# Edge counts of a two-layer graph network: gathering edges by groups of 12 target columns

## The chip, the cores and the metric

One core of a Trainium2 chip runs the kernel. The metric is device time of one execution in microseconds (us). Before the change it is 1008.47 us, the median of 3 runs (1006.94 to 1008.85). The engines are named as the profile names them: PE is TensorE (matmuls), PEld its weight loads, DVE VectorE, ACT ScalarE, POOL GpSimd, SP the queue that issues most transfers.

## The reference: what is computed

There are 625 nodes with 1024 features, and 20,000 edges (src, dst, type), sorted by dst, with 8 types. Layer 0 is an attention over edges, layer 1 a sum over types of means of neighbours, each followed by a residual and a layer norm.

```python
# layer 0
h = x @ W                                   # 625 x 1024
al, ar = h @ a[0, :D], h @ a[0, D:]
e = exp(-leaky_relu(al[src] + ar[dst], 0.1))
rowsum = segment_sum(e, src)
h_prime = segment_sum(e[:, None] * h[dst], src) / (rowsum[:, None] + 1e-5)
x = layernorm(x + elu(h_prime))
# layer 1
u = x @ root + bias
for r in range(8):
    mask = (edge_type == r)
    sums = segment_sum(x[src] * mask[:, None], dst)
    cnt = segment_sum(mask, dst)
    u = u + (sums / maximum(cnt, 1)[:, None]) @ weight[r]
z = concat([u, x], 1) @ w_gate + b_gate
x = layernorm(x + tanh(u) * z + x * (1 - z))
```

Every edge with the same (src, dst) contributes the same numbers, so the kernel never touches edges in the sums. It makes dense matrices of counts, C_r[src, dst], how often a pair occurs with type r. Layer 0 uses their sum over types, weighting by exp of the scores; layer 1 multiplies by C_r.

## The kernel before

The work is `fast` (from line 502). A scheduler places the recorded instructions of each engine, so their order follows readiness and not only the text. Nodes are held in five tiles of 128 rows, the last with 113 (`rows_of`).

**Start (lines 552 to 745).** dst, type and src of 78 x 256 edges come in on SP (677), the last 32 edges on the ACT queue (680), tile 0 of x on the ACT queue, W in eight chunks on SP (`load_w0`). VectorE turns them to two numbers an edge: the src, and a key that is type x window + (dst - first column of the window) (697 to 701). Four transposes on PE (707) and two copies (709) put edge number c x 128 + p into partition p, column c of `src2` and `key2`, each number twice.

**Counts (lines 747 to 884).** There are 157 chunks of 128 edges. As dst is sorted, the dst of a chunk lie near 4c, within a window of 12 to 24 columns (`LEADS`, `WINS`); edges outside are counted in `astray`, and if there is any, a general kernel runs afterwards. `one_hots` (764) makes, for four chunks at a time, `s_hot` (128 edges x 626: edge has src s; column 626 on is one) and `m_hot` (edge has type r and dst d in the window) with one f16 comparison each on VectorE. Nine such pairs of buffers are there (`HOTS`). `counts_of` (782) takes 64 dst columns at a time: for each of five src tiles it fills a bank of PSUM with 8 types x 64 columns by one matmul per chunk that can meet these columns, 1,030 in all, and ACT copies each bank into `cj` (803). For every 128 columns, `all_types` sums over types on VectorE and `store_counts` writes `cd` in DRAM, eight transfers by SP. `h_of` (747) computes h of a tile by 32 matmul passes; the loop at 855 places it between groups 0, 2, 4 and 6 of ten. `row_sums` (757) forms al and ar on VectorE from h. After group 7, ar is spread over all partitions (876, `p_ar`, and ACT's copy to `ar_b`); `scores_of` (820) then needs it, al and the counts.

**Attention (lines 887 to 1031).** `turn_scores` transposes scores on PE (843, `patt`) and ACT copies them to `attT`; `gather_h` (653, `phh`) multiplies with h for all 25 pairs of tiles. `attend` adds, normalizes and stores the new x, `turned_pieces` transposes and splits it in three pieces (h, l, d).

**Dense passes (from line 946).** `dense_tile` does x1 @ matrix in split precision, three matmuls per chunk (952, 953, 956), weights of 128 columns from the pieces, 512 columns of fp32r streamed. They run for root, the eight `weight[r]`, and the gate's two halves. For each r and half, 50 matmuls (1114, `pu`) multiply with the counts, fetched again from `cd`. The counts of edges per (dst, type) are the row of ones of `cd` (1059), cast by ACT (1060) and transposed (1065).

The few lines that a sentence can't say are those of the count matmul:

```python
nc.tensor.matmul(
    p3[:, :, lo - d0:hi - d0], s_hot[:k, c % BC, t * 128:(t + 1) * 128],
    m_hot[:k, c % BC, :R * win].rearrange("p (r w) -> p r w", r=R)[:, :, lo - base:hi - base],
    start=(i == 0), stop=(i == len(parts) - 1), skip_group_check=True)
```

Of the kernel before, what the change touches and what calls it, by code (L numbers as in the profile page):

```python
# [437 lines left out]

F32R = mybir.dt.float32r
SLOPES = 4  # L440
NC = -(-E // 128)
NROW = 78
LAST = E - NROW * 256
BC = 4
HOTS = 9
SONE = 626
G = 64
NG = -(-N // G)
H_AFTER = (0, 2, 4, 6)
AHEAD = 3  # L450
EARLY = 3
ST = 5
SP = ST * 128
# [6 lines left out]
def lead_of(b):  # L460

    first, last = b * BC / NC, min(1, (b + 1) * BC / NC)
    q = min(max(first, 0.5), last)
    return max(4, math.ceil(4.5 * N * math.sqrt(q * (1 - q) / E)))


LEADS = [lead_of(b) for b in range(-(-NC // BC))]
WINS = [SLOPES + 2 * lead for lead in LEADS]


def rows_of(t):
    return min(128, N - t * 128)
# [30 lines left out]
def fast(  # L503
# [26 lines left out]
    ps = ctx.enter_context(tc.tile_pool(name="f_ps", bufs=8, space=bass.MemoryType.PSUM))  # L530

    def bank(name):
        return ps.tile([128, 512], F32, tag="bank", name=name)
# [14 lines left out]
    def load_row(rows, ap, name):  # L548
# [15 lines left out]
                   allow_small_or_imprecise_dtypes=True)  # L564

    wins = const.tile([1, 2, NROW], F32, name="wins")
    lead_row, win_row = wins[:, 0, :], wins[:, 1, :]
    rows0 = 0
    while rows0 < NROW:
        lead = LEADS[2 * rows0 // BC]  # L570
        rows1 = rows0
        while rows1 < NROW and LEADS[2 * rows1 // BC] == lead:
            rows1 += 1
        nc.gpsimd.memset(lead_row[:, rows0:rows1], float(lead))
        rows0 = rows1
    nc.gpsimd.tensor_scalar(win_row, lead_row, 2.0, float(SLOPES), op0=OP.mult, op1=OP.add)
    first_row = const.tile([1, NROW], F32, name="first_row")
    nc.gpsimd.iota(first_row, pattern=[[2 * SLOPES, NROW]], base=0, channel_multiplier=0,
                   allow_small_or_imprecise_dtypes=True)
    nc.gpsimd.tensor_tensor(lead_row, first_row, lead_row, op=OP.subtract)  # L580
    p_win = bank("p_win")
    for i in range(2):
        nc.tensor.matmul(p_win[:NROW, i:i + 1], wins[:, i, :], ones[:1, :1], start=True, stop=True)
    row_wins = const.tile([128, 2], F32, name="row_wins")
    nc.vector.tensor_copy(row_wins[:NROW], p_win[:NROW, :2])
    row0, row_win = row_wins[:, 0:1], row_wins[:, 1:2]
# [9 lines left out]
    src2 = const.tile([128, NC, 2], F16, name="src2")  # L596
    key2 = const.tile([128, NC, 2], F16, name="key2")
# [23 lines left out]

    def tile_cols(t):
        return slice(t * 128, t * 128 + rows_of(t))

    def move_rows(n, dma):

        r0 = 0
        for m in (128, 112, 1):
            if m <= n - r0:
                dma(slice(r0, r0 + m))  # L630
                r0 += m
        assert r0 == n

    def load_x(pool, t, name, bufs=None, eng=nc.sync, clear=False):
        xt = pool.tile([128, D], F32, tag="x", name=f"{name}_{t}", bufs=bufs)
        if clear and rows_of(t) < 128:
            nc.gpsimd.memset(xt[96:], 0.0)
        xr = x[t * 128:t * 128 + rows_of(t), :]
        move_rows(rows_of(t), lambda rows: eng.dma_start(xt[rows], xr[rows]))
        return xt  # L640
# [12 lines left out]
    def gather_h(t, j):  # L653

        n, nj = rows_of(t), rows_of(j)
        for half in range(2):
            if j == 0:
                banks_h[t, half] = bank(f"phh_{t}_{half}")
            nc.tensor.matmul(banks_h[t, half][:n, :], attT[:nj, j, t * 128:t * 128 + n],  # L659
                             h_sb[:nj, j, half * HALF:(half + 1) * HALF],  # L660
                             start=(j == 0), stop=(j == ST - 1), skip_group_check=True)

    with tc.tile_pool(name="f_w", bufs=4, side="right") as wpool, \
# [7 lines left out]
        edge_rows = free[:NROW, D:D + 768].bitcast(I32).rearrange("p (i c) -> p i c", i=3)  # L671
        pair = free[:NROW, D + 768:D + 1280].rearrange("p (i c) -> p i c", i=2)
        rel, scratch = free[:NROW, D + 1280:D + 1536], free[:NROW, D + 1536:D + 1792]
        edge_last = scores.tile([1, 3, LAST], I32, name="edge_last")
        ends = ((1, dst), (2, etype), (0, src))
        for i, ap in ends:
            nc.sync.dma_start(edge_rows[:, i, :], ap[0:NROW * 256].rearrange("(p c) -> p c", c=256))
        x_next = load_x(xin, 0, "x", eng=nc.scalar)
        for i, ap in ends:
            nc.scalar.dma_start(edge_last[:, i, :], ap[NROW * 256:E].rearrange("(p c) -> p c", p=1))  # L680
# [15 lines left out]
        for h in range(2):  # L696
            nc.vector.tensor_scalar(rel[:, h * 128:(h + 1) * 128], edge_rows[:, 1, h * 128:(h + 1) * 128],
                                    row0[:NROW], float(-SLOPES * h), op0=OP.subtract, op1=OP.add)
        nc.vector.scalar_tensor_tensor(pair[:, 1, :], edge_rows[:, 2, :], row_win[:NROW], rel,
                                       op0=OP.mult, op1=OP.add)  # L700
        nc.vector.tensor_copy(pair[:, 0, :], edge_rows[:, 0, :])
        xT_next = x_turned(0)
        pe = bank("p_edges")
        pe4 = pe[:, :4 * NROW].rearrange("p (i h q) -> p i h q", i=2, h=2)
        for i in range(2):
            for h in range(2):
                nc.tensor.transpose(pe4[:, i, h, :], pair[:, i, h * 128:(h + 1) * 128], ident[:NROW, :NROW])
        for i, dst2 in enumerate((src2, key2)):
            nc.vector.tensor_copy(
                dst2[:, :2 * NROW, :].rearrange("p (q h) w -> p h q w", h=2),  # L710
                pe4[:, i, :, :].unsqueeze(3).to_broadcast([128, 2, NROW, 2]),
            )

        def last_edges():

            bad = scores.tile([NROW, 4], F32, name="bad")
            nc.vector.memset(bad, 0.0)
            pair_l = scores.tile([1, 2, LAST], F32, name="pair_l")
            rel_l = scores.tile([1, LAST], F32, name="rel_l")
            nc.vector.tensor_copy(pair_l[:, 0, :], edge_last[:, 0, :])  # L720
            nc.vector.tensor_scalar(rel_l, edge_last[:, 1, :], float(LEADS[-1] - SLOPES * (NC - 1)), None, op0=OP.add)
            nc.vector.scalar_tensor_tensor(pair_l[:, 1, :], edge_last[:, 2, :], float(WINS[-1]), rel_l,
                                           op0=OP.mult, op1=OP.add)
            pl = bank("p_last")
            for i in range(2):
                nc.tensor.matmul(pl[:LAST, i:i + 1], pair_l[:, i, :], ones[:1, :1], start=True, stop=True)
            for i, dst2 in enumerate((src2, key2)):
                nc.vector.tensor_copy(dst2[:LAST, NC - 1, :], pl[:LAST, i:i + 1].to_broadcast([LAST, 2]))
            for i, (bound, bound_l, op) in enumerate(((0.0, 0.0, OP.is_lt), (row_win[:NROW], float(WINS[-1]), OP.is_ge))):
                nc.vector.tensor_scalar(scratch, rel, bound, 0.0, op0=op, op1=OP.add, accum_out=bad[:, i:i + 1])  # L730
                nc.vector.tensor_scalar(scratch[:1, :LAST], rel_l, bound_l, 0.0, op0=op, op1=OP.add,
                                        accum_out=bad[:1, 2 + i:3 + i])
            pb = bank("p_bad")
            nc.tensor.matmul(pb[:1, :4], ones[:NROW, 0:1], bad, start=True, stop=True)
            total = scores.tile([1, 1], F32, name="total")
            nc.vector.tensor_reduce(total, pb[:1, :4], axis=AX.X, op=OP.add)
            nc.vector.tensor_copy(astray, total)

        built = {}
# [3 lines left out]
        s_hots = [hot.tile([128, BC, SP], F16, name=f"s_hot_{i}", bufs=1) for i in range(HOTS)]  # L743
        for m in s_hots:
            nc.gpsimd.memset(m[:, :, SONE:], 1.0)

        def h_of(t, xT):
            n = rows_of(t)
            halves_h = [bank(f"ph_{t}_{half}") for half in range(2)]
# [4 lines left out]
            for half, p in enumerate(halves_h):  # L754
                nc.scalar.copy(h_sb[:n, t, half * HALF:(half + 1) * HALF], p[:n, :])
# [8 lines left out]
        def one_hots(b):  # L764

            if b in built:
                return built[b]
            c0, n = b * BC, min(BC, NC - b * BC)
            k = 128 if c0 + n < NC else LAST
            if k == LAST:  # L770
                assert n == 1
            made = s_hots[b % HOTS], hot.tile([128, BC, R * max(WINS)], F16, tag="m_hot", name=f"m_hot_{b}")
# [82 lines left out]
        for g in range(NG):  # L855
# [5 lines left out]
            if g == 0:  # L861
                last_edges()
# [360 lines left out]
```

## Time and profile before

| what | us |
|---|---|
| median of 3 runs | 1008.47 |
| the profiled execution | 1009.31 |
| its span on the core | 1007.5 |
| from the start to the first count matmul | 0 to 24.8 |
| counts, and h of tiles 1 to 4 | 24.8 to 152.3 |
| attention, up to the first dense matmul | 152.3 to 196.8 |
| root passes | 196.8 to 256.1 |
| eight types | 256.1 to 878.4 |
| gate passes and end | 878.4 to 1007.5 |
| count matmuls (pc), busy | 62.4 |
| one-hots on VectorE, s_hot and m_hot, busy | 57.1 and 19.6 |

Times in views are us from the start of the span, unless marked ns. A group's line gives engine, operation, what is written and read, its shape and the number of instructions; then the busy time, the mean of one in ns, and the idle time of the engine just before them with what ended it. Instructions of one engine overlap in its pipeline, so the step from one start to the next can be shorter than the duration. The chain of waits is followed back from the last instruction to whatever released each; a piece counts both weight loads and matmuls. The TensorE clock was granted in full in each of these stages; the first matmuls ran at half pace (h passes of 854 ns until 13.3 us, 429 ns afterwards).

### The profile page before, as it was taken

Reading aid. Unit: us, or ns where it says so; the run is one execution under the profiler, and the core shown is the slowest. Engines: PE = TensorE matmul, PEld = TensorE weight load, DVE = VectorE, ACT = ScalarE, POOL = GpSimd, SP = SyncE. Lnnn points to the kernel's source line nnn. Section 1 sums busy time; section 2 is a strip of 40 time slices with the busy share of each in tenths; the row PEclk is TensorE's granted clock in tenths of the full one; section 3 lists DMA queues with packets and bytes.
Section 4 is the critical chain, followed back from the end, with each engine's and each line's share of the span. In section 5 each row is a group of like instructions: output and inputs, shape, how many; then the busy total and the mean of one; then the engine's idle time right before and its main releaser. Section 6 shows DMA issues by size and latency. Waiting matters only on the chain.

```text
span 1007.5 us, 12429 instructions
## 1 busy us (share of the span) xinstructions
PE 986.5 (98%) x4899; PEld 773.9 (77%) x4899; DVE 610.2 (61%) x948; ACT 393.4 (39%) x710; POOL 33.8 (3%) x72
## 2 busy tenths in 40 slices
PE   8999999999999999999999999999999999999994
PEld 4667774587888888888888888888888888888874
DVE  7477769876564563562653653644645635639995
ACT  1322337633445244343343442551551541423422
POOL 1000000100000000000000000000000000002123
PEclk9999999999999999999999999999999999999997
DMA  7022336453220220310310310311301202342212
GB/s 280 22 72 53 81 110 199 146 155 117 84 84 21 96 83 2 116 63 22 116 63 21 117 62 23 116 41 43 107 31 63 84 1 83 101 130 84 83 41 105
DMA packets 60951, 83.65 MB, mean 83 GB/s; under 512 B 28877, under 2 KB 29119, under 8 KB 60886
## 3 DMA queue, kind: packets, MB, share of 16 engines
q1 hardware_dynamic: 60735, 82.27, 25.5%
q8 instruction: 40, 0.66, 0.3%
q10 hardware_dynamic: 150, 0.52, 0.1%
q14 instruction: 26, 0.20, 0.1%
HBM read 71.11 MB, written 11.67 MB: 82 GB/s over the span
## 4 chain that ended last, share of the span: by engine, by line
PE 94%; DVE 3%; ACT 1%; issue 0%; DMA 0%; POOL 0%; SPq 0%; POOLq 0%; DVEq 0%; ACTq 0%
PE pu L1114 19%; PE p_w L956 14%; PE p_w L953 14%; PE p_w L952 14%; PE ph L752 7%; PE pc L799 5%; PE phh L659 4%; PE p_root L952 2%; PE p_root L956 2%; PE p_root L953 2%; PE p_wgx L956 2%; PE p_wgx L953 2%; PE p_wgx L952 2%; PE p_wgu L956 1%; PE p_wgu L953 1%; PE p_wgu L952 1%
## 5 line engine op out<-in xcount | busy, mean ns | idle before, releaser
L953 PE MATMUL p_w<-m_w,x_l 128*128 128x512 f32 x640 | 249.2, 390 | 0.0
L952 PE MATMUL p_w<-g_w,x_h 128*128 128x512 f32 x640 | 248.9, 389 | 0.0
L1114 PE MATMUL pu<-y,cf 128*128 128x512 f32 (+1 forms) x800 | 189.1, 395 | 0.0
L1114 PEld LDWEIGHTS pu<-y,cf 128*128 128x128 f32 (+1 forms) x800 | 150.6, 188 | 35.6
L1096 DVE SCALAR_TENSOR_TENSOR v<-p_w,v 128x512 f32<-128x512 f32 (+1 forms) x80 | 55.2, 689 | 202.1 <-PE p_w L956 153.0
L956 PE MATMUL p_w<-e_w,x_d 128*128 128x512 f32 x640 | 176.7, 390 | 0.0
L953 PEld LDWEIGHTS p_w<-m_w,x_l 128*128 128x128 f32 x640 | 120.1, 188 | 25.5 <-DVE m_w L926 0.2
L956 PEld LDWEIGHTS p_w<-e_w,x_d 128*128 128x128 f32 x640 | 120.1, 188 | 25.4 <-DVE e_w L927 0.3
L952 PEld LDWEIGHTS p_w<-g_w,x_h 128*128 128x128 f32 x640 | 120.1, 188 | 25.3
L1095 ACT ACTIVATE v<-p_w 128x512 f32<-128x512 f32 (+1 forms) x80 | 47.5, 593 | 217.2 <-PE p_w L953 217.2
L926 DVE SCALAR_TENSOR_TENSOR m_w<-raw_w,e_w 128x512 fp32r<-128x512 f32 x128 | 84.8, 683 | 36.2 <-ACT e_w L925 36.2
L1099 DVE TENSOR_TENSOR y<-v,y 128x512 fp32r<-128x512 f32 (+1 forms) x80 | 55.2, 690 | 50.8 <-ACT y L1098 50.8
L927 DVE TENSOR_TENSOR e_w<-g_w,m_w 128x512 fp32r<-128x512 f32 x128 | 84.7, 683 | 0.5
L924 ACT ACTIVATE g_w<-raw_w 128x512 fp32r<-128x512 f32 x128 | 73.1, 620 | 29.6 <-PE p_w L952 20.2
L1098 ACT CAST y<-v 128x512 fp32r<-128x512 f32 (+1 forms) x80 | 49.2, 615 | 75.2 <-DVE v L1096 75.2
L752 PE MATMUL ph<-w,xT 128*128 128x512 f32 (+1 forms) x160 | 72.8, 614 | 1.1 <-ACT xT L690 1.1
L925 ACT ACTIVATE e_w<-raw_w 128x512 fp32r<-128x512 f32 x128 | 73.0, 620 | 0.0
L799 PEld LDWEIGHTS <-s_hot 128*128 128x128 f16 x1030 | 62.0, 98 | 3.9 <-issue 3.7
L799 PE MATMUL pc<-m_hot,s_hot 128*128 128x192 f16 (+19 forms) x1030 | 62.4, 222 | 0.7 <-DVE m_hot L774 0.7
L774 DVE TENSOR_TENSOR s_hot<-iota,src 128x2504 f16<-128x2504 f16 (+1 forms) x40 | 57.1, 1429 | 9.4 <-PE pc L799 9.4
L752 PEld LDWEIGHTS ph<-w,xT 128*128 128x128 f32 (+1 forms) x160 | 30.7, 195 | 40.0 <-issue 38.0
L1118 DVE SCALAR_TENSOR_TENSOR L_gnn_bias_dram_u<-pu,inv,L_gnn_bias_dram_u 128x512 f32<-128x512 f32 (+1 forms) x80 | 55.5, 743 | 5.3 <-PE pu L1114 5.3
(155 smaller groups left out, 962.8 us busy)
## 6 DMA issues: line engine op xcount, KB each, us to landing
raw_w<-in_L_gnn_weight_dram SPq DMA_DIRECT2D x64, 512.0 KB, 3.3
cd<-cj SPq DMA_DIRECT2D x40, 160.0 KB, 3.6
cs<-cd SPq DMA_DIRECT2D x8, 800.0 KB, 5.6
w<-in_L_gnn_W_dram SPq DMA_DIRECT2D x8, 512.0 KB, 5.5
raw_root<-in_L_gnn_root_dram SPq DMA_DIRECT2D x8, 512.0 KB, 3.3
raw_wgx<-in_L_gnn_w_gate_dram SPq DMA_DIRECT2D x8, 512.0 KB, 3.4
raw_wgu<-in_L_gnn_w_gate_dram SPq DMA_DIRECT2D x8, 512.0 KB, 3.2
x<-in_x_dram SPq DMA_DIRECT2D x7, 512.0 KB
```

The lines of the kernel that those rows point to most:

```text
L752: nc.tensor.matmul(p[:n, :], xT[:, k, :n], w0_sb[k][:, half * HALF:(half + 1) * HALF], start=k == 0, stop=k == KC - 1)
L774: nc.vector.tensor_tensor(m[:k, :n, :width].rearrange("p c (j w) -> p c j w", w=2), iota16[:k, :width].rearrange("p (j w) -> p j w", w=2). ...
L799: nc.tensor.matmul(p3[:, :, lo - d0:hi - d0], s_hot[:k, c % BC, t * 128:(t + 1) * 128], m_hot[:k, c % BC, :R * win].rearrange("p (r w) -> ...
L924: nc.scalar.activation(g, w, AF.Copy, scale=DOWN)
L925: nc.scalar.activation(e, w, AF.Copy, scale=UP12 * DOWN)
L926: nc.vector.scalar_tensor_tensor(m, w, UP12, e.bitcast(F32), op0=OP.mult, op1=OP.subtract)
L927: nc.vector.tensor_tensor(e, g.bitcast(F32), m.bitcast(F32), op=OP.subtract)
L952: nc.tensor.matmul(p1[:n, :], h[:, k, :], g, start=k == 0, stop=False, skip_group_check=True)
L953: nc.tensor.matmul(p1[:n, :], l[:, k, :], m, start=False, stop=k == KC - 1, skip_group_check=True)
L956: nc.tensor.matmul(p2[:n, :], d[:, k, :], e, start=k == 0, stop=k == KC - 1, skip_group_check=True)
L1114: nc.tensor.matmul(p, c[:m, t, j * 128:(j + 1) * 128], piece[:m], start=(t == 0 and i == 0), stop=(t == ST - 1 and i == 1), skip_group_che ...
L1118: nc.vector.scalar_tensor_tensor(at, p[:n], inv[:n, j, r:r + 1], at, op0=OP.mult, op1=OP.add)
```

## The change

**Tiles.** All five tiles have 125 rows. Count matrices keep columns of 128 per tile, the last three clear. Matmuls and transposes use 125 rows and columns. Each transfer of a tile's rows is two now: 112 rows and 13.

**Start.** All edges come as 125 x 160, dst, src, type, two transfers each. VectorE packs each edge into one number, (dst x 40 + src tile x 8 + type) x 128 + src within its tile, in five operations; ACT's queue writes them to DRAM (`packed`, 627 rows of 32 with padding at both ends). For each of 55 groups of dst columns (eleven per tile, of 12 columns, the last of 5) a comparison of every 32nd dst and six small matmuls (`p_count`) tell at which block of 32 it begins. Eight indirect transfers on the POOL queue fetch for each group 16 blocks, as four chunks of 128 edges. `place_edges`, after seven of the eight steps of h of tile 0, transposes them, and four VectorE operations make `src2` and `key2`.

**Counts.** `s_hot` is 126 wide (src within its tile, whichever the tile; the last column is one), and `m_hot` has (dst column, src tile, type), 40 per dst column. One bank holds 12 dst columns x 40. A group takes four matmuls (two for the short one), 210 in all; chunks have fixed windows of columns 0 to 6, 1 to 11, 5 to 12 and 8 to 12. There are 15 builds of up to four groups, six comparisons each, five pairs of buffers. h of tiles 1 to 4 is cut in 32 steps, spread over the first 38 groups; x of a tile is transposed in the middle of h of the tile before. row sums, sums over types, the spread of ar and the first scores are put on a list with a due group each. PSUM has six banks for all else and two for h until the counts are done, then eight.

**Later.** The counts of edges per (dst, type) are the sum of five rows of `cd`, added on VectorE. Their total against 20,000 gives `astray` (a matmul `p_all`), in place of the four checks at the start.

The diff, cut to its core:

```diff
-SLOPES = 4
-NC = -(-E // 128)
...
-BC = 4
-HOTS = 9
-SONE = 626
-G = 64
-H_AFTER = (0, 2, 4, 6)
+TN = N // ST
+BLOCK = 32
+NBLOCK = E // BLOCK
+GCOLS = 12
+NG = -(-TN // GCOLS)
+NGS = ST * NG
+TR = ST * R
+LO = 128
+ONE = TN + 1
+BG = 4
+HOTS = 5
+H_GROUPS = 38
+LAG = 4
...
 def rows_of(t):
-    return min(128, N - t * 128)
+    return TN
...
-    ps = ctx.enter_context(tc.tile_pool(name="f_ps", bufs=8, space=bass.MemoryType.PSUM))
+    begin = ExitStack()
+    ps = [begin.enter_context(tc.tile_pool(name="f_ps0", bufs=6, space=bass.MemoryType.PSUM))]
+    ps_h = begin.enter_context(tc.tile_pool(name="f_ps_h", bufs=2, space=bass.MemoryType.PSUM))
...
     def move_rows(n, dma):
         r0 = 0
-        for m in (128, 112, 1):
-            if m <= n - r0:
-                dma(slice(r0, r0 + m))
-                r0 += m
+        for m in (n // 16 * 16, n % 16):
+            dma(slice(r0, r0 + m))
+            r0 += m
...
+        less = scores.tile([TN, per // BLOCK, 2 * NGS], F16, name="less")
+        nc.vector.tensor_tensor(
+            less, samples.unsqueeze(2).to_broadcast([TN, per // BLOCK, 2 * NGS]),
+            thr[:TN].rearrange("p g h -> p (g h)").unsqueeze(1).to_broadcast([TN, per // BLOCK, 2 * NGS]), op=OP.is_lt)
...
+        nc.vector.tensor_scalar(rest, edge_rows[:, 0, :], 1.0 / TN, 0.5 / TN - 0.5, op0=OP.mult, op1=OP.add)
+        nc.vector.tensor_scalar(rest, rest, MAGIC, MAGIC, op0=OP.add, op1=OP.subtract)
+        nc.vector.scalar_tensor_tensor(pack, rest, float(LO * R - TN), edge_rows[:, 0, :], op0=OP.mult, op1=OP.add)
+        nc.vector.scalar_tensor_tensor(pack, edge_rows[:, 1, :], float(LO * TR), pack, op0=OP.mult, op1=OP.add)
+        nc.vector.scalar_tensor_tensor(pack, edge_rows[:, 2, :], float(LO), pack, op0=OP.mult, op1=OP.add)
...
+        move_rows(TN, lambda rows: nc.scalar.dma_start(packed_rows[rows], pack[rows]))
+        p = bank("p_count")
+        for m in range(per // BLOCK):
+            nc.tensor.matmul(p[:2 * NGS, :1], less[:, m, :], ones16[:TN], start=m == 0, stop=False)
...
+        for b in range(2):
+            for i in range(4):
+                nc.gpsimd.indirect_dma_start(edges[:, b, i, :], None, packed[:, :],
+                                             bass.IndirectOffsetOnAxis(ap=at_block[:, b, i:i + 1], axis=0))
...
+        def place_edges():
+            pe = bank("p_edges")[:, :4 * NGS]
+            for b in range(2):
+                nc.tensor.transpose(pe[:, b * 2 * NGS:(b + 1) * 2 * NGS], edges[:, b].rearrange("p i c -> p (i c)"),
+                                    ident[:2 * NGS, :2 * NGS])
...
+            for b in range(-(-len(wins) // 2)):
+                equal(s_hot[:, b, :i1 - i0, :, :ONE].rearrange("p g h c -> p (g h) c"),
+                      src2[:, b, i0:i1].rearrange("p g h w -> p (g h) w"), ONE)
+            at = 0
+            for j, (first, end) in enumerate(wins):
+                width = TR * (end - first)
+                equal(m_hot[:, :i1 - i0, at:at + width], key2[:, j // 2, i0:i1, j % 2, :], width)
+                at += width
...
+        def counts_of(i, cj):
+            g = i % NG
+            s_hot, m_hot, _ = built[i]
+            p = bank(f"pc_{i}")
+            at = 0
+            for j, (first, end) in enumerate(WINS[g]):
+                nc.tensor.matmul(p[:, TR * first:TR * end], s_hot[:, j // 2, j % 2, :],
+                                 m_hot[:, at:at + TR * (end - first)],
+                                 start=j == 0, stop=j == len(WINS[g]) - 1, skip_group_check=True)
+                at += TR * (WINS[0][j][1] - first)
+            nd = cols_of(g)
+            nc.scalar.copy(cj.rearrange("s t r d -> s (t r) d")[:, :, g * GCOLS:g * GCOLS + nd],
+                           p[:, :TR * nd].rearrange("s (d q) -> s q d", q=TR))
...
+        for i in range(NGS):
+            while steps < min(n_steps, (i + 1) * n_steps // H_GROUPS):
+                next(h_steps, None)
+                steps += 1
+                if steps % KC == 0:
+                    due.append((i + (LAG if steps < n_steps else 0), row_sums, steps // KC))
+                    if steps == n_steps:
+                        due.append((i + 6, lambda _: spread_ar(), None))
...
+            counts_of(i, cjs[-1])
+            if i % NG == NG - 1:
+                due.append((i + LAG, counted, i // NG))
...
     def dense_tile(t, chunks, name):
-        n = 128
+        n = rows_of(t)
...
-    nc.sync.dma_start(ins16[:, :N], cd[:, SONE - 4 * 128, 4, :N])
-    nc.scalar.copy(ins[:, :N], ins16[:, :N])
+    nc.sync.dma_start(ins16, cd[:, ONE, :, :])
+    nc.vector.tensor_tensor(ins, ins16[:, 0, :], ins16[:, 1, :], op=OP.add)
+    for t in range(2, ST):
+        nc.vector.tensor_tensor(ins, ins16[:, t, :], ins, op=OP.add)
...
+    nc.vector.tensor_reduce(in_r, ins, axis=AX.X, op=OP.add)
+    p = bank("p_all")
+    nc.tensor.matmul(p[:1, :1], in_r, ones[:R, :1], start=True, stop=True)
+    nc.vector.tensor_scalar(astray, p[:1, :1], -1.0, float(E), op0=OP.mult, op1=OP.add)
```

## The prediction

> **What bounds the kernel now.** I read the page's busy line first, then the chain of work that ended last, then busy time by stage, then groups of instructions, then single stretches of the timeline.
>
> ```profile
> PE 986.5 (98%) x4899; PEld 773.9 (77%) x4899; DVE 610.2 (61%) x948; ACT 393.4 (39%) x710; POOL 33.8 (3%) x72
> ```
>
> TensorE (PE) is busy nearly all the time, but 98% is a mean; the chain says whether it is also what ends last where the change works (columns: start, length, what).
>
> ```profile
> 1.60 4.28 DMA attT<-in_src_dram
> 8.25 16.58 PE ph L752 x32
> 24.83 4.48 PE pc L799 x90
> 30.91 14.00 PE ph L752 x32
> ...
> 130.89 5.49 PE pc L799 x87
> 152.28 7.92 PE phh L659 x18
> ...
> 265.50 1.81 PE p_w L956 x8
> ```
>
> From 8 us on the chain is TensorE alone: products h (ph) and counts (pc) in turn, then the attention sum (phh), then the dense passes. So in this stretch a microsecond of TensorE is worth a microsecond, until another engine takes over. By stage (columns: window, length, busy PE, PEld, DVE, ACT, POOL, clock, DMA):
>
> ```profile
> 24.80:152.30 127.50, 125.12 (x1217) 90.85 (x1213) 86.17 (x111) 38.97 (x70) 0.60 (x1) 1.00 0.25 67
> 152.30:196.80 44.50, 44.50 (x126) 21.08 (x127) 42.17 (x73) 32.46 (x62) 4.24 (x7) 1.00 0.51 170
> ```
>
> In the count stage VectorE (DVE) has 41 us to spare, in the attention stage 2. The first dense product starts at 196.84; all sums below run up to that start, because what follows keeps its instructions.
>
> **The change part by part.** Rows that price it:
>
> ```profile
> L799 PE MATMUL pc<-m_hot,s_hot 128*128 128x192 f16 (+19 forms) x1030 | 62.4, 222 | 0.7 <-DVE m_hot L774 0.7
> L774 DVE TENSOR_TENSOR s_hot<-iota,src 128x2504 f16<-128x2504 f16 x39 | 56.7, 1453 | 9.4 <-PE pc L799 9.4
> L803 ACT CAST cj<-pc 128x512 f16<-128x512 f32 x45 | 26.4, 586 | 30.5 <-PE pc L799 30.5
> L659 PEld LDWEIGHTS phh<-h_sb,attT 128*128 128x128 f32 x64 | 11.8, 190 | 13.6 <-issue 11.7 <-ACT attT L845 1.3 <-ACT cj L803 0.2
> L659 PEld LDWEIGHTS phh<-h_sb,attT 128*113 128x113 f32 x16 | 2.8, 178 | 3.5 <-issue 3.5
> ```
>
> ```profile
> 9.68 1.44 DVE L774 TENSOR_TENSOR s_hot<-iota,src 128x2504 f16<-128x2504 f16 x1
> 11.05 0.34 DVE L774 TENSOR_TENSOR m_hot<-iota,key 128x384 f16<-128x384 f16 x1
> 11.31 1.45 DVE L774 TENSOR_TENSOR s_hot<-iota,src 128x2504 f16<-128x2504 f16 x1
> ```
>
> *Counts on TensorE, -37.7 us.* Away go 1,030 matmuls over 131,120 columns, 62.4 us. In come 50 groups of four (240, 400, 280, 160 columns) and 5 short ones (200, 160): 210 matmuls, 55,800 columns. Price between 0.442 ns a column (1.81 us for eight of 512, the chain's p_w piece) and 0.476 (62.4 / 131,120, which holds many narrow ones). The new ones are wide, so 0.442: 24.7 us (at most 26.6).
>
> *Interleaving, +2.8.* The changed program's order has 31 switches from counts to an h matmul before the last h; before there were none without transposes between. Where five 40-column counts (151.98) precede a phh (152.21) about 0.09 us goes beyond their streaming. 31 x 0.09 = 2.8. Bounds: 0, and 0.24 each (7.4), the gap before an h that waits for ACT's copy.
>
> *Turning x earlier, -1.5.* The four gaps before h (0.24 us, ACT's xT copy) fall away, with the six p_last and p_bad matmuls (0.44).
>
> *Start, +3.0.* Edges now come as six transfers, spaced about 0.4 us, then wait for a VectorE chain: the last is issued at 2.4, and lands 4.28 later (the chain's first line), 6.7. The order on VectorE puts the compare for the block counts behind the packing: five ops of 160 elements after the source ids, the last after the types (0.25 to 0.35 each, by the rows of 128 and 256 elements), compare of 550 elements 0.64, done 8.2. TensorE has the count of blocks (0.85, as p_win's four took 0.69) ahead of the x transposes, and ACT the write of the packed copy ahead of the xT copies. So transposes start at 9.1 instead of 4.29, h at 11.0 instead of 8.05. Below 2 or above 4.5 I don't expect it.
>
> *Gather, 0.* The packed write leaves at 7.6 and lands by 11.9 (4.28 again). Eight gathers on GpSimd follow; no row shows one. Bounds: 0.31 us each, SP's shortest issue of an edge load, and 4.28 each, one wholly after another. A gather of 110 rows is issued like a transfer, but by GpSimd, whose longest one-off op before this stage's end took 0.95; I take 0.95: 11.9 + 7.6 + 3.9 = 23.4. TensorE needs the edges after seven eighths of h of tile 0, at 11.0 + 14.8 = 25.8 (16.58 less an eighth of a warm h, 1.75); that h is the cover. From 1.25 us each the wait shows: at 4.28 the edges come at 46.1, +20.3. Behind the waiting transposes stand the rest of h and all counts.
>
> [...]
>
> *VectorE, 0 until the last h.* From the timeline an element of a one-hot costs (1.37 - 0.26) / (2504 - 384) = 0.523 ns, an instruction 0.06 us. Before: 124,618 elements, 80 instructions, 70 us. After: 27,720 + 59,400 = 87,120 elements, 90 instructions, 51 us. It starts later: at 27.9 instead of 9.7 (25.8, transposes 0.4, four key ops on 220 and 440 elements 1.6). Up to the last one-hot it also has four row sums (2.5 us each) and three sums over types (2.5): 51 + 10 + 7.5 ends at 96.4 if never waiting. TensorE's last h ends at 27.6 + 0.4 + 3.5 (turns) + 56.0 (four h) + 37 groups x 0.45 + 2.8 = 107. So it hides, with 10 us of cover.
>
> *A new stall, +5.3.* Before, three of ten groups' counts (17 us) stood between the last h and the first attention transposes and covered row sums, ar's spread and the first scores. Now 18 short groups, 8.1 us, stand there. The road from the last h: two copies 1.4, row sums 2.5, p_ar 0.6, ACT behind seven evictions and two copies to 5.8; then VectorE's 1.40 (types of tile 3) and six score ops of 0.735, one of 0.74, one more 0.8: first turned scores at 12.2; with ACT's copies behind a pair of weight casts phh begins at 14.0. Idle: 14.0 - 8.1 - 0.6 of transposes = 5.3. Next late would be the pieces of x1 for the first dense tile. TensorE has 46.9 us from phh's begin (100 passes at 0.429, 36 transposes at 0.109). VectorE has, from there, 14.9 us of scores and types, 18 weight pieces and small ops 12.3, three tiles of x1 13.1, the pieces 2.4: 42.7. They stay hidden by 4 us, as before by 3 (ready at 193.0, used from 196.0). ACT's evictions now write runs of 12 in another order; no row shows that form: 0.586 by the old one; twice that would add 11 here.
>
> *Tiles of 125, 0.* Instructions keep their count and width in the free dimension. 3,440 dense and aggregation matmuls lose 3 of 128 weight columns. The load shrinks with columns (190 to 178 ns for 113), 2.4 ns for 3, and lies beneath a 227 ns matmul. Bounds: -8.3 us if the load sets the pace, and +24 if an uneven layout costs the 6.9 ns by which pu (11.66 us for 50) exceeds p_w.
>
> [...]
>
> *Edges' sums later, +0.3.* Four VectorE adds and a reduction (3.7 us) stand in place of one ACT cast; the load came 7.8 us before its use, and that slack covers them; the p_all matmul remains. The 28 extra transfers (112 + 13 rows) go to SP, which waits hundreds of us for free buffers; without that cover some 0.4 us each.
>
> Sum: 3.0 - 37.7 + 2.8 - 1.5 + 5.3 + 0.3 = -27.8. The profiled execution took 1009.31 (span 1007.5), 0.84 above the median of 1008.47: 981.5 for it, 980.7 for the median.
>
> **Rivals.** [...] (2) *ACT takes over after the last h* with slow evictions: for: runs of 12; against: ACT is 30% busy. 992. (3) *125 columns cost*: for: pu's 6.9 ns; against: equal ph pace at 113 and 128 columns (429 ns). 1004. (4) *Slower*: the one-hots lose VectorE's f16 pace, as smaller blocks with another layout. f32 rows cost 0.735 us for 640 elements, 1.15 ns, over twice 0.523. At twice, +45.6; 10 hidden, 35.6 - 27.8 = +7.8: 1016. It decides from 38 us more, 0.96 ns an element. Against: every operand stays f16 in pairs. (5) *Better*: the load sets the pace: 972.
>
> **How the numbers follow.** Forecast 0.60, gather 0.16, ACT 0.07, columns 0.05, one-hots 0.05, better 0.07. The likeliest gives 981, its own range 974 to 988. To leave out no more than 2 in 10: 971 to 996. What a measurement here can tell from no change is about 0.2%, 2 us. Slower takes the one-hot case and two of the columns', 0.07; within 0.2%, 0.02; faster the rest, 0.91.
>
> **What would show it.** pc near 25 us in 210 matmuls; h at about 11; p_edges transposes without a wait; the last h near 107; a gap of some 5 us before phh; the first dense matmul near 169; p_w still at 227 ns. Wrong if TensorE waits at p_edges, if VectorE is full before the last h, or if p_w's pace moved.

## The result and the profile after

The changed kernel took 994.81 us (median of 4 runs, 993.65 to 995.49), the kernel before beside it 1007.81 (1006.94 to 1008.85): 0.9869 of it, 95% interval 0.9852 to 0.9886. It is 13.0 us faster. The forecast was 981, a gain of 27.8; the time lies inside the stated 971 to 996, close to the upper end, and 13.0 of the 27.8 us came. The profiled execution took 993.65, its span is 991.8.

The first view is the chain of work that ended last (start, length, what).

```profile
2.03 4.02 DMA attT<-in_src_dram
8.09 6.26 DMA packed<-attT
24.81 3.20 DMA edges<-packed,at_block
28.39 2.76 PE ph L773 x4
...
120.01 1.98 PE phh L678 x4
...
253.83 1.87 PE p_w L1016 x8
255.70 11.67 PE pu L1182 x50
...
293.50 1.87 PE p_w L1016 x8
295.36 11.67 PE pu L1182 x50
```

Two things are to be seen. At the start the chain runs through the packed copy and the gather (it did not before), and the edges land at 28.0. In the dense part eight products in a row take 1.87 us; they took 1.81 before. The aggregation (pu) takes 11.67, as before. From one pu to the next there are 39.67 us in place of 38.90. The chain of the kernel before:

```profile
283.64 11.66 PE pu L1114 x50
322.54 11.66 PE pu L1114 x50
```

The groups of instructions say the same (out<-in, weights rows*columns, count, then busy time and mean ns of one). The first line is of the kernel before, the others are of after, the counts (pc) among them:

```profile
L956 PE MATMUL p_w<-e_w,x_d 128*128 128x512 f32 x640 | 176.7, 390 | 0.0
...
L1182 PE MATMUL pu<-y,cf 125*125 125x512 f32 x800 | 189.2, 394 | 0.0
...
L823 PE MATMUL pc<-m_hot,s_hot 128*128 128x240 f16 (+2 forms) x210 | 29.5, 277 | 0.0
...
L1016 PE MATMUL p_w<-e_w,x_d 128*125 128x512 f32 x640 | 180.3, 394 | 0.0
```

The mean of a p_w record is 394 ns (390 before); the records are pipelined, so the pace is read from the starts: 233.3 ns from one p_w matmul to the next, 226.7 before (most frequent steps 233 and 234 against 227 and 226). In the same way the 210 count matmuls, busy for 29.5 us by their records, take 24.1 us from each start to the next start on TensorE; the 1,030 before took 62.0.

Stages by the same borders as in the forecast, in us:

| | before | after | difference |
|---|---|---|---|
| start to the first dense product | 196.84 | 166.84 | -30.0 |
| first dense product to the end | 810.7 | 825.0 | +14.3 |
| of this, 16 half passes over a type | 16 x 38.90 | 16 x 39.67 | +12.3 |
| span | 1007.5 | 991.8 | -15.7 |

(The medians differ by 13.0 and not by 15.7, because the profiled execution of before was 1.5 above the median of its runs now and that of after 1.2 below its own.) So the stage that the change rewrites gained 2.2 us more than forecast, and the stage of which the forecast said that nothing changes gave 14.3 back. The 2.2 is no more than scatter: of six profiled kernels with this same front (after and five of the kernels below) the first dense product starts between 166.75 and 169.21, and the forecast was 169.04.

What TensorE waited for in the whole of the execution after (engine, line, releaser: us in total, times, longest):

```profile
PE p_count L730 <- DVE less L717: 8.8, 1, 8.8
PE patt L869 <- DVE e L859: 2.8, 1, 2.8
PE p_edges L747 <- DMA edges<-packed,at_block: 2.3, 2, 1.6
PE p_wgu L1016 <- DVE e_wgu L985: 1.4, 2, 0.9
PE phh L678 <- ACT attT L871: 0.4, 1, 0.4
```

No count waits for a one-hot, the gather is late by 2.3 us, and the stall behind the last h is 2.8 + 0.4.

### The profile page after: what moved, and what is told of

Read it like the earlier page. It is cut to its first block, busy times and chain, and to the rows that moved or that the text cites. A ratio compares the mean times of both kernels' runs of the same rounds, so it can differ in the third digit from the quotient of the medians.

```text
span 991.8 us, 10873 instructions
## 1 busy us (share of the span) xinstructions
PE 964.9 (97%) x4075; PEld 721.4 (73%) x4075; DVE 596.0 (60%) x955; ACT 391.5 (39%) x714; POOL 43.5 (4%) x73
## 4 chain that ended last, share of the span: by engine, by line
PE 93%; DVE 3%; DMA 1%; POOL 1%; ACT 1%; issue 1%; SPq 0%; POOLq 0%; ACTq 0%; DVEq 0%
PE pu L1182 19%; PE p_w L1016 15%; PE p_w L1012 15%; PE p_w L1013 15%; PE ph L773 6%; PE phh L678 4%; PE p_root L1016 2%; PE p_root L1012 2%; PE p_wgx L1013 2%; PE p_root L1013 2%; PE p_wgx L1016 2%; PE p_wgx L1012 2%; PE pc L823 2%; PE p_wgu L1016 1%; PE p_wgu L1013 1%; PE p_wgu L1012 1%
## 5 line engine op out<-in xcount | busy, mean ns | idle before, releaser
L1012 PE MATMUL p_w<-g_w,x_h 128*125 128x512 f32 x640 | 252.0, 394 | 0.0
L1013 PE MATMUL p_w<-m_w,x_l 128*125 128x512 f32 x640 | 252.0, 394 | 0.0
L1182 PE MATMUL pu<-y,cf 125*125 125x512 f32 x800 | 189.2, 394 | 0.0
L1016 PE MATMUL p_w<-e_w,x_d 128*125 128x512 f32 x640 | 180.3, 394 | 0.0
L1182 PEld LDWEIGHTS pu<-y,cf 125*125 125x125 f32 x800 | 148.1, 185 | 38.5
L1013 PEld LDWEIGHTS p_w<-m_w,x_l 128*125 128x125 f32 x640 | 118.5, 185 | 31.1 <-DVE m_w L984 0.2
L1016 PEld LDWEIGHTS p_w<-e_w,x_d 128*125 128x125 f32 x640 | 118.4, 185 | 31.2 <-DVE e_w L985 0.2
L1012 PEld LDWEIGHTS p_w<-g_w,x_h 128*125 128x125 f32 x640 | 118.4, 185 | 30.7
L773 PE MATMUL ph<-w,xT 128*125 128x512 f32 x160 | 78.9, 622 | 0.0
L1186 DVE SCALAR_TENSOR_TENSOR L_gnn_bias_dram_u<-pu,inv,L_gnn_bias_dram_u 125x512 f32<-125x512 f32 x80 | 55.5, 742 | 7.9 <-PE pu L1182 7.9
```

What stands on the lines that cost most here:

```text
L773: nc.tensor.matmul(p[:n, :], xT[:, k, :n], w0_sb[k][:, half * HALF:(half + 1) * HALF], start=k == 0, stop=k == KC - 1)
L1012: nc.tensor.matmul(p1[:n, :], h[:, k, :n], g, start=k == 0, stop=False, skip_group_check=True)
L1013: nc.tensor.matmul(p1[:n, :], l[:, k, :n], m, start=False, stop=k == KC - 1, skip_group_check=True)
L1016: nc.tensor.matmul(p2[:n, :], d[:, k, :n], e, start=k == 0, stop=k == KC - 1, skip_group_check=True)
L1182: nc.tensor.matmul(p, c[:m, t, j * 128:j * 128 + n], piece[:m], start=(t == 0 and i == 0), stop=(t == ST - 1 and i == 1), skip_group_check ...
L1186: nc.vector.scalar_tensor_tensor(at, p, inv[:n, j, r:r + 1], at, op0=OP.mult, op1=OP.add)
```

## The experiments

### Is it the 125 weight columns?

*wide* clears (on GpSimd) the three spare columns of every piece and uses all 128 as weights in the dense matmuls.

```diff
+        for i in (h, l, d):
+            nc.gpsimd.memset(i[:, :, n:].bitcast(F32), 0.0)
-            nc.tensor.matmul(p1[:n, :], h[:, k, :n], g, ...)
+            nc.tensor.matmul(p1, h[:, k, :], g, ...)
```

> The changed kernel with the three spare columns of each piece of x1 and u cleared by GpSimd, and all 128 used as weights in the 2,640 dense matmuls; the aggregation (pu) stays at 125. Columns theory (125 weight columns cost each dense matmul 233.3 - 226.9 = 6.4 ns): eight second products in a row take 1.81 us again instead of 1.87, 16.9 us go, some 978 us. Rival (the dense passes are slower for another reason: more transfers, the earlier start, the clock): the pace stays at 1.87 and the time at 995.

979.98 us (5 runs), 0.9726 of before [0.9712, 0.9741]: 14.8 less than the changed kernel. *widepu* does the same for the aggregation, where the spare columns of the counts are zero already.

```diff
-                p = banks_u[j][:n]
+                p = banks_u[j]
-    nc.tensor.matmul(p, c[:m, t, j * 128:j * 128 + n], piece[:m], ...)
+    nc.tensor.matmul(p, c[:m, t, j * 128:(j + 1) * 128], piece[:m], ...)
```

> The kernel of the run above, with 128 weight columns in the 800 aggregation matmuls (pu) too; the last three columns of the counts are zeros. If their 233.3 ns after the change is the price of 125 columns, as the dense ones', up to 800 x 6.4 = 5.1 us more go, some 973 us, and 50 take about 11.35 us. If they are slow for their own reason, as before the change with 128 columns (11.66 for 50), nothing more goes: 978 us.

976.25 us, 0.9686 [0.9666, 0.9705]: 3.7 more (in the traces half a pass falls from 38.88 to 38.59 us, 16 of them 4.6). The chains of both, *wide* first:

```profile
254.12 1.81 PE p_w L1018 x8
255.93 11.66 PE pu L1184 x50
```

```profile
251.96 1.81 PE p_w L1018 x8
253.77 11.36 PE pu L1184 x50
```

The pace follows the edit, line by line: 1.87 to 1.81 for the dense products with the first, 11.66 to 11.36 for the aggregation with the second. Neither more transfers nor the earlier start nor the clock is needed, and three more columns, all zeros, are worth 18.6 us together. In this code the weight columns of a product are also the rows that it writes in PSUM (`p1[:n, :]`), so the edit widens both; no run separates the two. The theory stands so far; that each matmul of 125 columns has its price does not follow yet.

### Is it a price of each matmul?

*before125* takes the kernel before and leaves the last three columns out of seven dense matmuls in eight.

```diff
+            w = 125 if k else 128
-            nc.tensor.matmul(p1[:n, :], h[:, k, :], g, ...)
+            nc.tensor.matmul(p1[:w, :], h[:, k, :w], g, ...)
```

> The kernel before, whose dense matmuls use the first 125 columns from k = 1 on (the products of the last three rows of each tile are left out there): this part of the change alone. Columns theory: 2,640 x 7/8 = 2,310 matmuls at 6.4 ns are 14.8 us more, 1022 us. Rival (it only costs together with the rest of the change): 1008.

1010.01 us, 1.0026 [1.0017, 1.0036]. Only 2.4 of 14.8 us came, so the price for each matmul falls. *k0wide* is the other side of it: the changed kernel with 128 columns for k = 0 alone.

> The changed kernel, of whose dense matmuls only those with k = 0, one in eight, use 128 weight columns; the others stay at 125. If each matmul with 125 columns costs 6.4 ns: 330 x 6.4 = 2.1 us less than the changed kernel, 993 us. If the slow pace is a lock that one wider matmul breaks (before, with 125 columns from k = 1 on, gained only 2.4 us in place of 14.8): most steps at 227 ns, some 981 us.

985.03 us, 0.978 [0.9765, 0.9795]: one matmul in eight, made wider, takes away 9.8 of the 14.8 us. In the profiled executions, from the first dense product to the end, it is 12.2 of 15.6 (824.9 us after, 812.7 here, 809.4 in *wide*). The chain of *k0wide* inside one pass (the first three lines are the first tile of a pass, where three kinds of product alternate, the others two later tiles):

```profile
620.19 0.23 PE p_w L1020
620.43 0.23 PE p_w L1015
620.66 0.23 PE p_w L1016
...
627.56 1.81 PE p_w L1020 x8
633.00 1.81 PE p_w L1020 x8
```

By the records, a pass there has some twenty steps of 233 ns in the first tile and then steps of 227 to its end, for the same 125 columns. In *before125* four steps in five are 226 or 227 as well. So the same 125-column product goes at either pace. Not every wider matmul ends the slow one: the three at the head of the first tile have 128 columns too, and the pace changes only where the second tile begins.

*widths* changes the columns of the second product alone (k from 1 on), beside neighbours of 128; in *purewidths* all dense matmuls of one type have one width.

```diff
+    WID = [128, 127, 126, 125, 124, 120, 112, 96]
+        w = wid_of(name)
+        h, l, d = (i[:, :, :w] for i in x1[t])
```

> The kernel with 128 dense columns, but the second product of type r uses, from k = 1 on, only the first 128, 127, 126, 124, 120, 112, 96 and 64 columns of its weights for r = 0 to 7 (the rest of those products is left out). If 128 alone is fast, the eight second products in a row take 1.81 us for type 0 and some 1.87 for all others. If odd numbers, or numbers that 4 or 16 do not divide, are slow: 1.87 for 127 (and 126, 124, 120 as far as it goes) and 1.81 for the rest. If the load's length counted, they would grow shorter with the columns.

> The kernel with 128 dense columns; in the dense matmuls of type r all weights have 128, 127, 126, 125, 124, 120, 112 and 96 columns for r = 0 to 7 (the products of the other rows are left out, and so are those rows in the aggregation of that type). Theory A (only 128 columns are fast): 227 ns for type 0, 233 or more for all others. Theory B (the pace is a lock between load and matmul, which some widths fall into): as in the mixed run, 227 for 128, 127 and 124, and some 233 for 126, 125 and 120.

980.96 and 987.99 us, one execution each, so only the steps inside them are read. The mean step from start to start, in ns, from the records of p_w (128 of *purewidths* is its second half pass, as the first holds single steps of up to 338):

| columns | 128 | 127 | 126 | 125 | 124 | 120 | 112 | 96 | 64 |
|---|---|---|---|---|---|---|---|---|---|
| all matmuls of the pass (*purewidths*) | 226.8 | 233.3 | 233.3 | 233.3 | 226.8 | 233.3 | 229.0 | 230.1 | - |
| seven in a row (k from 1) among 128 (*widths*) | 226.7 | 226.7 | 233.6 | - | 226.7 | 233.3 | 228.9 | 230.0 | 230.0 |

The chain of *purewidths*, one line each from the types with 128, 127 and 125 columns:

```profile
277.07 1.81 PE p_w L1023 x8
...
316.20 1.87 PE p_w L1023 x8
...
474.84 1.87 PE p_w L1023 x8
```

127 columns are slow by themselves and fast beside 128; 124 are as fast as 128 in both; 120 are slower than 112; and 64 columns are no faster than 128. So neither "only 128 is fast" nor "fewer columns, shorter load" holds, and theory B fails on 127. What the runs show for 120 to 128 columns is a pace of a whole run of matmuls, near 226.7 or near 233.3, that goes on until something breaks it, and into which some widths fall; 112 to 64 columns lie between, at 229 to 230. Why these widths, and what in TensorE holds the pace, no run here tells; that stays open.

### What was the late gather worth?

*afterlate* is the changed kernel with the edges placed later: their transposes stand behind the whole h of tile 0 and the turning of tile 1, and six steps of h come before the first counts (the other 26 are spread over the same 38 groups).

```diff
-            if k == KC - 2:
-                place_edges()
+        place_edges()
+        for _ in range(H_FIRST):
+            next(h_steps)
```

> The changed kernel, 125 columns as it is, with nothing but the edges' transposes placed later: behind all of h of tile 0 and the turning of tile 1, six h steps ahead of the first counts. The late gather's price by itself: 2.3 us of wait, less 1.3 that the run with 128 columns still showed, and the half clock that followed it, some 1.7 us. Theory: 2.7 to 4 us less, 991 to 992 us. Rival (VectorE's one-hots begin no earlier and pace the stage): 995.

990.3 us, 0.9820 [0.9807, 0.9834]: 4.5 less, a little over the upper end of what was expected. Timelines of TensorE, after and then *afterlate* (start, length, instruction, and the wait ahead of it in brackets):

```profile
26.17 0.29 PE L747 MATMUL p_edges<-ident,edges 110*128 110x110 f32 x1 [0.64 <-DMA edges<-packed,at_block]
28.11 0.28 PE L747 MATMUL p_edges<-ident,edges 110*128 110x110 f32 x1 [1.65 <-DMA edges<-packed,at_block]
28.23 2.92 PE L773 MATMUL ph<-w,xT 128*125 128x512 f32 x4
```

```profile
24.46 3.17 PE L774 MATMUL ph<-w,xT 128*125 128x512 f32 x7
27.47 1.02 PE L668 MATMUL px<-ident,x 125*128 125x125 f32 x8
28.32 0.35 PE L748 MATMUL p_edges<-ident,edges 110*128 110x110 f32 x2
```

In the second the wait is gone. In the first, four h take 2.92 us right behind it, where four in the steady stretch start within 1.75. The windows from 28 to 33 us show why (busy PE, PEld, DVE, ACT, POOL, then the granted clock, the DMA share and GB/s), after and then *afterlate*:

```profile
28.00:33.00 5.00, 4.89 (x14) 2.87 (x15) 4.43 (x9) 2.06 (x4) 0.00 (x0) 0.66 0.00 0
```

```profile
28.00:33.00 5.00, 5.00 (x18) 2.57 (x17) 4.61 (x10) 1.22 (x3) 0.00 (x0) 1.00 0.31 102
```

The clock was at half from 28.96 to 32.37 us, 3.41 us, which costs 1.7 by estimate, half of it. Wait and clock together make 4.0, and in the traces the last h starts 4.2 earlier (103.00 against 107.18). The first dense product starts only 2.9 earlier (163.96 against 166.84), since in *afterlate* the clock was at half from 114.71 to 118.13 us, around the begin of the attention; what is left of the 4.5 lies behind that start. VectorE, whose one-hots begin no earlier, was not in the way.

*late* is the same on top of *widepu*:

> The kernel with 128 columns in dense and aggregation (976 us), with the transposes of the edges placed behind all of h of tile 0 and the turning of tile 1, and six h steps behind them ahead of the first counts. If the late gather cost the path its 2.3 us of wait and the half clock after it (4 h in 2.92 us in place of 1.75, some 1.4 us with the transposes): 3.7 us go, 972.5. Rival (VectorE's one-hots, which begin no earlier, set the pace up to the last h): 976.

971.21 us, 0.9647 [0.9634, 0.9661], 5.0 below *widepu*; 3.7 were expected.

### What stands behind the last h?

*late30* spreads h over 30 groups of counts (`H_GROUPS = 30`), *late36* over 36.

> The same, with the h steps spread over 30 groups of counts instead of 38, so that some 25 groups lie behind the last h instead of 17. If the 3.2 us that TensorE waits between the last h and the attention sum are the road from the last h (row sums, ar, scores), they are covered by 3.5 us more of counts: 970. Rival (VectorE, 11.1 of 12 us busy there, is what ends it, and only gets its one-hots later): no gain over the run above, 972.5 to 975.

978.64 us, 0.9727 [0.9714, 0.9741]: 7.4 more. The cover was there, but TensorE now waited for what makes the counts:

```profile
PE pc L824 <- DVE m_hot L800: 4.0, 3, 2.7
PE pc L824 <- ACT cj L829: 2.2, 1, 2.2
```

The clock fell behind these waits: it was at half from 113.95 to 127.60 us, 13.65 us, against 3.41 (116.61 to 120.03) in *late*. The attention sum begins 6.7 us later (122.89 against 116.20); how much of that is waits and how much clock, no run separates.

> 128 columns everywhere, edges late (971 us), with h over 36 groups in place of 38: two groups of counts more (0.9 us) behind the last h, whose road to the attention sum left TensorE idle for 2.8 us. Theory (a little of that idle time can be covered before VectorE runs out of one-hots): 970 to 971. Rival (VectorE is at its limit at 38 already, as with 30): over 972.

970.6 us, 0.9636 [0.9623, 0.9649], the best of all kernels here, but not distinguishable from *late*; the wait for the scores is still 2.8. What makes the counts becomes the limit somewhere between 36 and 30 groups. So two runs took the sums over types of tiles 0 and 1 off VectorE (`eng = nc.gpsimd if j < 2 else nc.vector`), with h over 38 and over 33 groups.

> The kernel with the edges placed late (971 us), whose sums over types of tiles 0 and 1 (2.8 us each) run on GpSimd instead of VectorE; h stays spread over 38 groups. Theory: VectorE is not on the path before the last h, so nothing changes: 971. Rival (VectorE already paces the counts): 5.6 us off VectorE shorten the stage, down to 967; or GpSimd's long adds hold VectorE up: above 973.

> The same with h spread over 33 groups. With 30 groups the run took 7.4 us more, since TensorE waited 6 us behind the last h for one-hots and the evictions after them. Theory (VectorE's sum of work sets the attention sum's begin): with 5.6 us moved off it, the earlier last h brings 2 to 3 us, 968. Rival (ScalarE's evictions, or GpSimd's pace, end it): 971 or more.

977.82 and 975.04 us, 0.9713 [0.9689, 0.9737] and 0.9676 [0.966, 0.9692]: 6.6 and 3.8 more than *late*. Timelines of *latepool38*, GpSimd and then VectorE:

```profile
59.06 8.12 POOL L838 TENSOR_TENSOR c<-cj 128x2500 f16<-128x2500 f16 x1 [33.14 <-ACT cj L829]
```

```profile
58.61 1.26 DVE L800 TENSOR_TENSOR s_hot<-iota,src 128x1008 f16<-128x1008 f16 x2
...
62.91 7.50 DVE L800 TENSOR_TENSOR s_hot<-iota,src 128x756 f16<-128x756 f16 x2 [0.52 <-PE pc L824]
```

Two smaller compares take 7.50 us where two larger ones took 1.26; by the records the first (0.55 us elsewhere) ends at 67.59, just behind GpSimd's add (67.19), and the second runs beside GpSimd's next two adds. The same is seen beside the other three adds of this form in the two runs: a compare that comes in behind the add's start ends 0.35 to 0.52 us behind its end. The other three adds take 5.0 to 5.3 us; the one of 8.12 began while VectorE was in a row of compares, which kept their usual lengths to their end at 62.40. In *latepool38* VectorE's compares beside GpSimd's adds took 15.9 us more than their usual lengths, against the 5.6 it was spared, and TensorE waited 5.3 us for its row sums; its clock was at half twice for 3.41 us, once in *late*. In *latepool33* TensorE waited 5.4 us for ScalarE's copies, with 6.83 us at half clock. The theories of both were wrong, the rivals (GpSimd's adds hold VectorE up; 971 or more) right.

## Why the prediction was wrong, point by point

- *Start, +3.0.* Right: h begins at 11.25 (forecast 11.0).
- *Counts, -37.7, and interleaving, +2.8.* The first is right (24.1 us for the new counts, forecast 24.7) and the second was not there. From the turning of tile 1 (done at 32.66) to the end of the last h (107.61) lie 74.95 us. Less 56.0 for h and 2.6 for turning three tiles, 16.3 are left for some 37 groups of counts and all switches; the forecast had 37 x 0.45 + 2.8 = 19.5.
- *Gather, 0.* Wrong by 4.0 as above: the edges came at 28.0, not 23.4. The packed write took 6.26 us and not 4.28, and the first gather was issued at 15.50, where the forecast had the write landed at 11.9. (The DMA engines were busy for 0.84 of the first 28 us; whether that made the write slow, no run tells.) The eight follow one another by 1.31 (1.0 of issue, 0.30 between), a little more than the 1.25 from which the forecast let the wait show: by its own sum, 0.5 us of wait. The landing took 3.20; the forecast's 3.9 had no row. So most of the wait came from the late write. The forecast named a wait at p_edges among the signs that it is wrong and gave a late gather 0.16; the longer issue which that chance was reckoned with is shown by no run. At 1.31 us an issue, 2.3 of wait with 1.7 of clock came.
- *VectorE, 0 until the last h.* Right. No count waited for a one-hot, and the last h ended at 107.6 (forecast 107).
- *A new stall, +5.3.* Right in kind, smaller: TensorE waits 3.2 us, and phh begins 12.4 us behind the last h, not 14.0.
- *Edges' sums, +0.3.* No wait of TensorE's is put down to them.
- *Tiles of 125, 0.* This is the step that failed. Up to the first dense product the sum was 2.2 us too cautious (166.84 against 169.04); behind it 14.3 us came that the sum had at nothing. With 128 columns, and nothing else changed, the kernel takes 979.98: 1.0 from the forecast. That closeness is luck in part: up to the first dense product the gather's +4.0 is hidden by switches, stall and attention, which came out 3.2, 1.6 and 1.2 us below the forecast.

The reasoning of that step was that the load (185 to 188 ns) lies beneath the matmul, so that its columns cannot matter. The load does lie beneath (its records are 185 ns at 125 columns and 188 at 128), and the columns matter all the same: uniform 125 columns hold the passes at 233.3 ns. The equal pace of h at 113 and 128 columns, named against the rival, is true again after the change (56.0 us of h, 0.4375 each), but h multiplies f32 and the passes fp32r, and there it did not hold (233.3 ns at 125 columns, 226.7 at 128). The rival "125 columns cost" had the mechanism's place and its size for one matmul (6.9 ns; measured 6.6); its 1004 was too much, since pu was at that pace already and since the front did better. It was given 0.05, with a bound of +24 written beside it: that bound rested on a row of the same type in the same kernel, and the evidence against it on another type. That the size agrees is luck in part, too: before the change pu had 128 weight columns, and its steps went from 224 to 242 ns with a mean of 233.2; afterwards they are 233 and 234. In *widepu*, with 128 columns and 125 rows in every tile, they are 226 and 227, so the 11.66 us of before were not a price of 125 columns. Before, some of these matmuls had 113 rows and the rest 128; no run tells whether that made them uneven.

The load's own time does not tell the widths apart either: its records hardly differ (185 ns at 125 columns, 188 at 128), 124 columns go at 226.8 ns, and 127 at 226.7 beside wider ones.

## What to carry to other kernels

A matmul whose load is hidden can still change pace with the shape of its weights (here 233.3 ns with 125 columns, 226.7 with 128): where thousands of them follow one another, price a new width from a row of the same type and width, or keep the width that runs well and fill the spare columns with zeros. Here a wait of TensorE cost its own length and in some runs clock behind it (an estimated 1.7 us for the 3.41 at half behind the gather's 2.3 of wait; 13.65 at half in *late30*, where 6.2 us of waits followed one another), so a late input is better met by moving work ahead of it than by its average arrival. Work moved to an idle engine is not free if it lengthens the instructions of the one that paces (beside GpSimd's add two compares took 7.50 us, and two larger ones before them 1.26): look at the length of the neighbour's instructions, not only at its share of busy time.

## What the runs showed of the hardware

- With 120 to 128 weight columns the fp32r pace has two values, near 226.7 and 233.3 ns for 512 elements, and can hold over whole passes (112 and 96 columns: 229.0 and 230.1); one wider matmul in eight moves most of a pass from the slow one to the fast (*k0wide*: 39.02 us a half pass, against 39.67 and 38.88 in *wide*).
- Behind the first rise of the clock, all stretches between two changes of it are, in these traces, whole multiples of 3.413 us: 1, 2 (*k0wide*, *latepool33*) or 4 (*late30*) at half clock, from 2 (*latepool38*) to 289 (*before125*) at full. Laid on this grid, the 14 traces part as follows (busy means records of weight loads and matmuls). In each of the 28 stretches at full clock that half clock followed, 14 of them at the end of the program, TensorE was busy for at most 0.45 of the 3.413 us; in every other it was busy for 0.46 or more. From half it rose behind stretches busy for 0.94 or more, and stayed behind 0.80 or less.
- So a wait need not cost clock. After the same 2.77 us of waiting for the scores, *wide* had a spell from 121.1 to 124.5 (0.45 busy in the stretch ahead of it) and the changed kernel none (0.52 and 0.56); the first dense product started at 168.85 in the one and 166.84 in the other.
- VectorE's f16 compares and GpSimd's f16 adds held each other up: a compare of 0.55 us took 4.68 and ended just behind the add, and an add took 8.12 us where others took 5.0 to 5.3. Why, no run shows.
- An indirect transfer of 110 rows occupied GpSimd's queue for 1.31 us, the last landing 3.2 us behind the start of its issue.
